# Summing a scan's states in pairs: one addition on GpSimd for every two transposes on TensorE, and all products with C on VectorE

## The chip, the cores and the metric

The kernel runs on one core of one Trainium2 chip. The time is device time in microseconds (us) of one execution, and the figure given is the median of several. An execution that the hardware profiler recorded is the source of everything said about single instructions; its page gives engines short names: PE for TensorE's matmuls, PEld for its weight loads, DVE for VectorE, ACT for ScalarE, POOL for GpSimd, SP for the engine that issues the DMAs.

## The reference, cut to what matters

Two layers of a network on x of shape (4, 512, 512). The change lies in layer 0's first half, a selective state-space scan with 512 channels, 512 time steps and 16 states:

```
delta = softplus(dt_proj_w @ dt_lo + dt_proj_b)       # per channel and time
def step(state, (d_t, B_t, C_t, u_t)):
    dA    = exp(d_t[..., None] * A)                   # A: channel x state
    state = state * dA + (d_t * u_t)[..., None] * B_t[:, None, :]
    y_t   = einsum('ben,bn->be', state, C_t)          # sum over the 16 states
y = (y + D * u) * silu(layernorm(x));   x = x + tanh(g_xattn[0]) * y^T
```

After it come a ternary feed-forward block ("bitnet"), cross attention with 16 heads, and four experts, each added to x behind its own gate.

## The kernel before, in words

**Batches and stages.** The four batch elements go through the kernel one behind the other. Batch 0's scan and bitnet run alone at the start. From then on the attention of batch b (16 heads, a head's query, score and weighted-sum steps staggered over three heads) is traced together with layer 0 of batch b+1, that is `front(b+1)`, `scan(b+1)` and `bitnet(b+1)`; a rate constant says how many steps of layer 0 come per step of attention. Beside the last batch's attention run the experts of batches 0 to 2, and the experts of batch 3 end the kernel. So there are four scan stages; in the last three attention shares every engine.

**Who sets the order.** The engines each work off a queue in order. The kernel's source is only traced: a scheduler at build time orders each engine's queue by priority (the order of tracing) and by when its own model of times expects operands and buffers to be there. A change in one place therefore moves instructions in others.

**The scan.** For a batch, 16 states n by four groups t of 128 channels make 64 tiles of 128 x 512 (channel by time). For each, `scan` (L606 to L686) does this: ScalarE writes dA = exp(delta * A) into a PSUM bank (L652); GpSimd writes h = (delta u) * B (`pool_mult`, L656, recorded at the helper's line L186); VectorE scans along time (L659 or L662); the state is multiplied by C, a row broadcast into the tile `cc`; and TensorE adds the product's transpose to y (`add`, four matmuls of 128x128 at L627 into PSUM tiles `py`). The choice of engine for the product with C:

```
if (G * n + t) % 8 in of_8:
    nc.vector.tensor_tensor_scan(dA, dA, h, 0.0, ALU.mult, ALU.add)
    nc.vector.tensor_tensor(h, dA, cc, ALU.mult)
else:
    nc.vector.tensor_tensor_scan(h, dA, h, 0.0, ALU.mult, ALU.add)
    pool_mult(h, h, cc)
```

With `DVE_OF_8` VectorE takes six products in eight (L660) and GpSimd two in eight (L186); batch 0 is called with `range(7)`, seven in eight, and with four channel groups at a time, the others with G = 2. In the first branch the state stays in PSUM until the product has read it; in the second the scan writes to SBUF, and dA's bank is free when the scan ends.

**Buffers.** `pss` has four PSUM banks; with G = 2 two hold `py`, so two are left for dA and for `psz`. SBUF tiles of 128 x 512 come from classes with the numbers of `MIDS`: class "v" holds h, and also tiles of `front`, the normalised rows, and in the last batch's attention the exponentials `pr`; class "t" holds the four tiles s1 of `front`'s softplus (L593), the skip term's tiles `udr` (L634, added to y after state 2), `zth` and `acc` of the scan, batch 0's `hq` and `xs`, and the rows `exr` of the early experts (L1158). A tile waits until the one that held its buffer has been read for the last time.

**Attention's small steps on GpSimd.** Between the scan's products stand the inverse square roots `rk` and `rqs` (`rsqrt`, L183), the low halves `ks` (L889) and some `hl` (L991), which keys and softmax wait for. VectorE's `hl` (L992) has two operands in SBUF.

Of the kernel before, what the change touches and what calls it, by code (L numbers as in the profile page):

```python
# [35 lines left out]
ALU = mybir.AluOpType  # L36
# [10 lines left out]
DS = 16  # L47
# [16 lines left out]
DVE_OF_8 = (0, 1, 2, 4, 5, 6)  # L64


MIDS = {"g": 5, "v": 6, "t": 4, "q": 2, "n": 1, "x": 1, "y": 2}
FILL0 = 4
RATE_S = 0.5
RATE_B = 0.8  # L70
# [21 lines left out]
SC = 4  # L92
PT = 3
MT = 0
AV = 4
VB = 2
WB = 5
# [13 lines left out]
def flamingo_kernel(  # L111
# [8 lines left out]
    nc = tc.nc  # L120
# [9 lines left out]
    pss = ctx.enter_context(tc.tile_pool(name="pss", bufs=4, space=PSUM))  # L130

    def psum(pool, name, tag="m", bufs=None):
        if tag == "a":
            role = name.rstrip("_0123456789")
            if pool is psa and role in LAST_PSS and name[len(role)] == str(B - 1):
                return psum(pss, name)
            tag = ATAG.get(role, "m")
            bufs = ABUF[tag]
        kw = {} if bufs is None else {"bufs": bufs}
        return pool.tile([P, 512], F32, tag=tag, name=name, **kw)  # L140
# [12 lines left out]
    def midt(shape, dtype, name, tag):  # L153
        if tag in wider:
            pool, bufs = wider[tag]
            return pool.tile(shape, dtype, tag=f"m{tag}", name=name, bufs=bufs)
        return mid.tile(shape, dtype, tag=tag, name=name, bufs=MIDS[tag])

# [18 lines left out]
    def load_x(b):  # L177
        x_sb[b] = xpool.tile([P, T, L], F32, tag="x", name=f"x{b}", bufs=2)
        nc.sync.dma_start(x_sb[b], x[b].rearrange("(p t) f -> p t f", t=T))
# [5 lines left out]
    def pool_mult(out, a, b):  # L185
        nc.gpsimd.tensor_tensor(out, a, b, ALU.mult)  # L186

    def row_stats(xr, name, gain=1.0, res=None):

        st = sm(6, f"bst{name[0]}", f"bst{name}", 2)  # L190
        nc.vector.bn_stats(st, xr)
        mv = sm(2, f"mv{name[0]}", f"mv{name}")
        nc.vector.bn_aggr(mv, st)
        var = sm(1, f"var{name[0]}", f"var{name}")
        nc.vector.tensor_scalar(var, mv[:, 1:2], EPS, gain**-2, ALU.add, ALU.mult)
        if res is None:
            res = sm(2, f"rst{name[0]}", f"rst{name}")
        rsqrt(res[:, 0:1], var)
        nc.vector.scalar_tensor_tensor(res[:, 1:2], mv[:, 0:1], -1.0, res[:, 0:1], ALU.mult, ALU.mult)
        return res  # L200

    def normed(xr, stats, name, tag="v"):
        xn = midt([P, L], F32, f"xn{name}", tag)
        if name[0] in NRMD:
            nc.vector.tensor_scalar(xn, xr, stats[:, 0:1], stats[:, 1:2], ALU.mult, ALU.add)
        else:
            nc.scalar.activation(xn, xr, AF.Identity, bias=stats[:, 1:2], scale=stats[:, 0:1])
        return xn
# [306 lines left out]
    def transposed(pool, src, name, g=None):  # L515

        ps = psum(pool, name).rearrange("p (t e) -> p t e", t=T)
        for t, s in enumerate(src):
            nc.tensor.transpose(ps[:, t, :], s[:, g::T], ident)
        return ps[:, : len(src), :]  # L520
# [82 lines left out]
            pool_mult(u[t], delta[t], u[t])  # L603
        yield

    def scan(b, of_8=DVE_OF_8, G=2, y_tile=lambda name: psum(pss, name), between=lambda n, ins: None):  # L606
        delta, du, ud_d, bd = fronts[b]
        sz_d = dram.tile([P, T, L], F32, tag="szd", name=f"szd{b}", bufs=2)

        def silu_z(t):  # L610

            xt = x_sb[b]
            w = normed(xt[:, t, :], row_stats(xt[:, t, :], f"z{b}{t}", 0.5), f"z{b}{t}")
            th = midt([P, L], F32, f"zth{b}{t}", "t")
            nc.scalar.activation(th, w, AF.Tanh)
            nc.vector.scalar_tensor_tensor(w, th, 1.0, w, ALU.add, ALU.mult)
            return w

        for t0 in range(0, T, G):
            gs = T // G
            ys = [y_tile(f"py{b}{t0}{i}").rearrange("p (g t e) -> p g t e", g=gs, t=G) for i in range(G)]

            def add(src, t, first, last):
                for g in range(T):
                    nc.tensor.matmul(  # L627
                        ys[g // gs][:, g % gs, t, :], src[:, g::T], ident, is_transpose=True,
                        start=first and t == 0 and g % gs == 0, stop=last, skip_group_check=True,
                    )  # L630

            uds, szs = [], []
            for t in range(G):
                uds.append(midt([P, L], F32, f"udr{b}{t0}{t}", "t"))  # L634
                nc.sync.dma_start(uds[t], ud_d[:, t0 + t, :])
            for n in range(DS):
                if n == 4 and x_sb[b] is None:
                    while b >= 2 and estats[b - 2] is None:
                        yield
                    load_x(b)  # L640
                if n == SZR and t0 > 0:
                    for t in range(t0, t0 + G):
                        szs.append(midt([P, L], F32, f"szr{b}{t}", "v"))
                        nc.sync.dma_start(szs[-1], sz_d[:, t, :])
                bc = midt([P, L], F32, f"bc{b}{t0}_{n}", "g")
                nc.sync.dma_start(bc, bd[n, :].partition_broadcast(P))
                cc = midt([P, L], F32, f"cc{b}{t0}_{n}", "g")
                nc.sync.dma_start(cc, bd[DS + n, :].partition_broadcast(P))
                for t in range(G):
                    nm = f"{b}{t0}{t}_{n}"  # L650
                    dA = psum(pss, f"dA{nm}")
                    last = nc.scalar.activation(  # L652
                        dA, delta[t0 + t], AF.Exp, scale=A[:, t0 + t, n : n + 1]
                    )
                    h = midt([P, L], F32, f"h{nm}", "v")
                    pool_mult(h, du[t0 + t], bc)  # L656
# [4 lines that stand above are left out]
                    else:  # L661
                        nc.vector.tensor_tensor_scan(h, dA, h, 0.0, ALU.mult, ALU.add)  # L662
                        pool_mult(h, h, cc)
                    add(h, t, n == 0, n == DS - 1)
                    if n == 2:
                        add(uds[t], t, False, False)
                between(n, last.ins)
                yield

            xt = x_sb[b]  # L670
            if t0 == 0:
                szs = [silu_z(t) for t in range(T)]
                for t in range(G, T):
                    nc.sync.dma_start(sz_d[:, t, :], szs[t])
            for g in range(T):
                if g % gs == 0:
                    acc = midt([P, gs, G, P], F32, f"acc{b}{t0}{g}", "t")
                    nc.scalar.copy(acc, ys[g // gs])
                ps = transposed(pss, szs[:G], f"psz{b}{t0}{g}", g)
                a = acc[:, g % gs]  # L680
                nc.vector.tensor_tensor(a, a, ps, ALU.mult)
                xv = xt[:, g, :].rearrange("q (p e) -> q p e", e=T)[:, :, t0 : t0 + G]
                nc.vector.scalar_tensor_tensor(
                    xv, a.rearrange("q e p -> q p e"), tg[:, 0:1], xv, ALU.mult, ALU.add
                )
                yield  # L686
# [139 lines left out]
    def attention(b):  # L826
# [70 lines left out]
        def values(hg):  # L897
            def v_tile(shape, dtype, name):
                return at.tile(shape, dtype, tag="v", name=name, bufs=AV)

# [270 lines left out]
    def last_experts(pool, places):  # L1171
# [12 lines left out]
        for t in (T - 1, *range(T - 1)):  # L1184
            xTs[t] = pool.tile([P, 2, T, P], F16, tag="v", name=f"lxT{t}", bufs=AV)
            split_normed(x_sb[b][:, t, :], estats[b][t], xTs[t], slice(0, P), f"l{t}", "q")
# [22 lines left out]
    with tc.tile_pool(name="pro", bufs=1) as pro, tc.tile_pool(name="psp", bufs=4, space=PSUM) as psp:  # L1209
# [8 lines left out]

        if MT:
            wider["t"] = pro, MT  # L1220

# [14 lines left out]
        def between(n, ins):  # L1236

            if n < 0:
                for _ in range(4):
                    next(side)  # L1240
            for _ in range(2 if 0 <= n < SIDE1 else 0):
                with tc.issue_after(ins):
                    next(side, None)

        run(front(0, inp, between))
        run(scan(0, range(7), 4, iter_ps, between))
        wider.clear()
        for _ in side:
# [50 lines left out]
    n = B * NH  # L1299
    for i in range(-2, n):  # L1300
        b2, h2 = divmod(i + 2, NH)
# [11 lines left out]
        q = steps[b2](h2, 0) if i + 2 < n else iter(())  # L1313
# [100 lines left out]
```

## Time and profile before

| what | value |
|---|---|
| median of three runs | 2029.95 us (2026.92 to 2033.11) |
| the profiled execution | 2033.82 us, span 2032.0 us |
| busy | PE 80%, DVE 76%, ACT 65%, POOL 46% of the span |
| mean granted TensorE clock | 0.877 |
| h products with B on POOL, L186 | 256 of 1327 ns |
| products with C on POOL, L186 | 56 of 1304 ns |
| products with C on DVE, L660 | 200 of 677 ns |
| scans on DVE | L659 200 of 1217 ns, L662 56 of 1207 ns |
| transposes of h on PE, L627 | 1024 of 341 ns, weight loads 1024 of 214 ns |

The scan's instructions lie from 50 to 200 us (batch 0), 380 to 600 (batch 1), 720 to 980 (batch 2) and 1100 to 1390 (batch 3). An instruction's mean duration is from its start to its end as recorded; neighbours on an engine overlap a little, so a group's sum can exceed the time that it takes. A wait is given as idle time of an engine before an instruction, with the instruction that ended it.

### The profile page before, as it was taken

How to read it: one execution, taken by the hardware profiler on the slowest of the kernel's cores; microseconds unless marked ns; L12 is line 12 of the kernel's file. 1: busy time of each engine (PE TensorE's matmuls, PEld its weight loads, DVE VectorE, ACT ScalarE, POOL GpSimd, SP SyncE). 2: the span in 40 equal slices, each digit the busy share in tenths (PEclk: the TensorE clock that was granted, in tenths of full speed). 3: DMA queues.
4: the chain of work that ended last, by engine and by line, in shares of the span. 5: the costliest groups of instructions: out<-in, count | busy, mean ns of one | idle time of the engine just before them, and what ended most of it. 6: DMA issues, size and time to landing. Idle time of an engine off the chain costs nothing. (4 is left out here: it accounts for less than half of the span.)

```text
span 2032.0 us, 27171 instructions
## 1 busy us (share of the span) xinstructions
PE 1634.5 (80%) x8366; PEld 901.1 (44%) x8366; DVE 1536.9 (76%) x2893; ACT 1328.6 (65%) x3121; POOL 937.3 (46%) x931
## 2 busy tenths in 40 slices
PE   4354976667879986779898887788999879798888
PEld 1343322344544444455443554554444445454456
DVE  4898865998998787898986885999764564654654
ACT  5797566765757886465658664756565676766763
POOL 1886112784744268475414782775133431412211
PEclk8555987768889998899999989899999889898989
DMA  7553558687884588775435777676445686866754
GB/s 258 185 161 133 151 158 242 185 228 218 231 214 107 132 216 182 191 177 155 106 87 149 199 180 191 156 170 146 91 103 111 139 228 158 210 160 165 193 138 140
DMA packets 516322, 342.50 MB, mean 169 GB/s; under 512 B 425800, under 2 KB 427976, under 8 KB 510032
## 3 DMA queue, kind: packets, MB, share of 16 engines
q1 hardware_dynamic: 516176, 340.77, 64.2%
q8 instruction: 65, 1.06, 0.2%
q14 instruction: 81, 0.66, 0.1%
HBM read 193.10 MB, written 44.30 MB: 117 GB/s over the span
## 5 line engine op out<-in xcount | busy, mean ns | idle before, releaser
L186 POOL TENSOR_TENSOR h<-u,bc 128x512 f32<-128x512 f32 x256 | 334.7, 1327 | 94.5 <-DMA bc<-bd 43.8
L627 PE MATMUL py<-ident,h 128*128 128x128 f32 x1024 | 201.1, 341 | 123.7 <-DVE h L660 101.9
L252 PE MATMUL ps<-kT,qT 128*128 128x512 f16 x768 | 217.0, 406 | 66.5 <-ACT pr L971 51.9
L652 ACT ACTIVATE dA<-delta,A 128x512 f32<-128x512 f32 x256 | 172.6, 685 | 138.8 <-DVE h L660 103.0
L659 DVE TENSOR_TENSOR_SCAN dA<-dA,h 128x512 f32<-128x512 f32 x200 | 240.8, 1217 | 23.5 <-POOL h L186 15.0
L252 PE MATMUL pav<-pT,v 128*128 128x256 f16 x1536 | 215.7, 297 | 46.2 <-DMA pT<-hl 28.9
L627 PEld LDWEIGHTS py<-ident,h 128*128 128x128 f32 x1024 | 167.6, 214 | 167.7 <-DVE h L660 131.0
L951 DVE TENSOR_REDUCE nmx<-ps 128x1 f32<-128x512 f32 x256 | 172.2, 679 | 54.9 <-PE ps L252 54.6
L971 ACT ACTIVATE pr<-ps,nmx,rqs 128x512 f32<-128x512 f32 x256 | 197.7, 775 | 20.8 <-DVE hl L992 16.6
L992 DVE SCALAR_TENSOR_TENSOR hl<-pr,den,hl 128x512 f16<-128x512 f32 x214 | 185.2, 882 | 33.4 <-ACT hl L989 17.0
L252 PEld LDWEIGHTS <-v 128*128 128x128 f16 x1536 | 161.7, 106 | 103.2 <-issue 44.2
L252 PE MATMUL pq<-axnT,wq 128*128 128x512 f16 x768 | 194.1, 404 | 7.7 <-DMA axnT<-xsa 3.1
L252 PE MATMUL pwo<-wo,oT 128*128 128x512 f16 x768 | 181.1, 386 | 8.6 <-DVE oT L244 3.6
L991 POOL TENSOR_SCALAR hl<-pr,den 128x512 f16<-128x512 f32 x86 | 66.3, 771 | 203.5 <-issue 97.5
L252 PEld LDWEIGHTS <-qT 128*128 128x128 f16 x768 | 77.8, 104 | 156.4 <-issue 88.6
L183 POOL TENSOR_TENSOR rqs<-ssq,mhalf 128x4 f32<-128x4 f32 x64 | 68.4, 1068 | 161.9 <-ACT ssq L940 149.0
L252 PEld LDWEIGHTS <-cT 128*128 128x128 f16 x768 | 79.1, 106 | 128.8 <-issue 61.7
L660 DVE TENSOR_TENSOR h<-dA,cc 128x512 f32<-128x512 f32 x200 | 133.7, 677 | 2.5 <-PE py L627 0.5
L252 PEld LDWEIGHTS <-wq 128*128 128x128 f16 x768 | 80.1, 105 | 108.3 <-issue 36.0
L252 PE MATMUL pk<-wk,cT 128*128 128x512 f16 x384 | 110.1, 432 | 19.9 <-DMA wk<-dwk 11.9
L252 PEld LDWEIGHTS <-oT 128*128 128x128 f16 x768 | 74.8, 100 | 100.6 <-issue 10.6
L989 ACT ACTIVATE hl<-pr,den 128x512 f16<-128x512 f32 x128 | 91.8, 717 | 36.3 <-DVE den L978 28.6
(386 smaller groups left out, 3478.2 us busy)
## 6 DMA issues: line engine op xcount, KB each, us to landing
bc<-bd SPq DMA_DIRECT2D x112, 256.0 KB
cc<-bd SPq DMA_DIRECT2D x112, 256.0 KB
wq<-dwq SPq DMA_DIRECT2D x64, 256.0 KB
wo<-dwo SPq DMA_DIRECT2D x64, 256.0 KB
w<-w3d SPq DMA_DIRECT2D x12, 1024.0 KB
de<-hle SPq DMA_DIRECT2D x9, 1024.0 KB
lw<-de SPq DMA_DIRECT2D x18, 512.0 KB
wk<-dwk SPq DMA_DIRECT2D x16, 512.0 KB
```

The costliest lines, as they stand in the source:

```text
L183: nc.gpsimd.tensor_tensor(res, arg, mhalf[:, : arg.shape[1]], ALU.pow)
L186: nc.gpsimd.tensor_tensor(out, a, b, ALU.mult)
L252: nc.tensor.matmul(ps, l, r, start=first and i == 0, stop=last and i == n - 1)
L627: nc.tensor.matmul(ys[g // gs][:, g % gs, t, :], src[:, g::T], ident, is_transpose=True, start=first and t == 0 and g % gs == 0, stop=last ...
L652: last = nc.scalar.activation(dA, delta[t0 + t], AF.Exp, scale=A[:, t0 + t, n : n + 1])
L659: nc.vector.tensor_tensor_scan(dA, dA, h, 0.0, ALU.mult, ALU.add)
L660: nc.vector.tensor_tensor(h, dA, cc, ALU.mult)
L951: nc.vector.tensor_reduce(nmx[:, c : c + 1], ps, AX.X, ALU.max, negate=True)
L971: mark[0] = nc.scalar.activation(pr, scs[c], AF.Exp, bias=nmx[:, one], scale=rqs[:, one], accum_out=den[:, c - c0 : c - c0 + 1],).ins
L989: nc.scalar.activation(hl[:, c, 0], prs[c], AF.Copy, scale=den[:, one])
L991: nc.gpsimd.tensor_scalar(hl[:, c, 0], prs[c], den[:, one], 1.0, ALU.mult, ALU.mult)
L992: nc.vector.scalar_tensor_tensor(hl[:, c, 1], prs[c], den[:, one], hl[:, c, 0], ALU.mult, ALU.subtract)
```

## The change

In batches 1 to 3 the products of states n = 2k and 2k+1 are kept for each channel group, GpSimd adds the second to the first, and TensorE transposes only the sum into y, 8 times per channel group instead of 16. The skip term is added after the second pair. `of_8` becomes `range(8)` for these batches, so that VectorE takes all products with C there. Batch 0 keeps its seven in eight and its single sums. Class "v" has seven buffers instead of six, class "t" three instead of four.

```diff
-MIDS = {"g": 5, "v": 6, "t": 4, "q": 2, "n": 1, "x": 1, "y": 2}
+MIDS = {"g": 5, "v": 7, "t": 3, "q": 2, "n": 1, "x": 1, "y": 2}
...
+PAIRS = (1, 2, 3)
...
-    def scan(b, of_8=DVE_OF_8, G=2, y_tile=lambda name: psum(pss, name), between=lambda n, ins: None):
+    def scan(b, of_8=range(8), G=2, y_tile=lambda name: psum(pss, name), between=lambda n, ins: None):
...
-            uds, szs = [], []
+            uds, szs, odd = [], [], [None] * G
...
-                    add(h, t, n == 0, n == DS - 1)
-                    if n == 2:
-                        add(uds[t], t, False, False)
+                    if b not in PAIRS:
+                        add(h, t, n == 0, n == DS - 1)
+                        if n == 2:
+                            add(uds[t], t, False, False)
+                    elif n % 2 == 0:
+                        odd[t] = h
+                    else:
+                        h2 = odd[t]
+                        nc.gpsimd.tensor_tensor(h2, h2, h, ALU.add)
+                        add(h2, t, n == 1, n == DS - 1)
+                        if n == 3:
+                            add(uds[t], t, False, False)
```

The lines of the changed kernel behind the constants lie one lower, behind this block ten lower; the addition is at L673.

## The prediction

> **What bounds the kernel now.** I read the page first for each engine's share, then the busy time of the three stretches in which a scan of batches 1 to 3 runs beside attention, then the waits inside them, then a few single rows. The page says that no engine is full over the whole span:
>
> ```profile
> PE 1634.5 (80%) x8366; PEld 901.1 (44%) x8366; DVE 1536.9 (76%) x2893; ACT 1328.6 (65%) x3121; POOL 937.3 (46%) x931
> L627 PE MATMUL py<-ident,h 128*128 128x128 f32 x1024 | 201.1, 341 | 123.7 <-DVE h L660 101.9
> L660 DVE TENSOR_TENSOR h<-dA,cc 128x512 f32<-128x512 f32 x200 | 133.7, 677 | 2.5 <-PE py L627 0.5
> ```
>
> That average mixes stages. The busy times of the scan stretches of batches 1, 2 and 3 (columns: stretch, its length, then busy us of PE, PEld, DVE, ACT, POOL, the granted clock, the DMA share, GB/s):
>
> ```profile
> 380.00:600.00 220.00, 160.89 (x797) 102.81 (x795) 207.06 (x320) 143.37 (x360) 143.16 (x123) 0.78 0.82 223
> 720.00:980.00 260.00, 206.68 (x1108) 127.98 (x1107) 221.20 (x356) 168.35 (x423) 175.97 (x160) 0.90 0.73 179
> 1100.00:1390.00 290.00, 235.30 (x1241) 140.85 (x1239) 239.05 (x382) 184.28 (x467) 184.97 (x169) 0.91 0.74 180
> ```
>
> VectorE leads in each: 94%, 85% and 82% of the stretch, against TensorE's 73%, 79% and 81%. Only the first is clearly VectorE's. The bitnet stretches between them are TensorE's (118.4 of 120 us from 600 to 720 us), but no transposes of h stand there. The waits in the first stretch, of TensorE, VectorE and GpSimd:
>
> ```profile
> PE py L627 <- DVE h L660: 21.5, 11, 5.8
> POOL h L186 <- PE py L627: 18.8, 7, 7.3
> POOL h L186 <- DVE h L662: 18.7, 8, 4.3
> PE ps L252 <- ACT pr L971: 15.7, 5, 5.8
> ...
> DVE nmx L951 <- PE ps L252: 9.3, 7, 3.1
> ```
>
> TensorE stands in its queue before a transpose whose product VectorE hasn't finished, with attention's matmuls behind it; and most of VectorE's little idle time (9.3 of 12.9 us) is spent on scores that come late.
>
> **The change, part by part.** *Products with C.* 48 of them (16 per stage) go from GpSimd to VectorE, each 677 ns by L660, so 10.8 us per stage and 32.5 us in all. How much of it ends up on the path I take from VectorE's share of each stage: 10.8 x (0.94 + 0.85 + 0.82) = +28.2 us. The bounds are 0, if its idle time took everything, and +32.5 us.
>
> *Transposes.* 384 matmuls with their weight loads go, 128 per stage (256 become 128; the skip term's stay). Their recorded mean of 341 ns overlaps with neighbours; back to back the trace has this:
>
> ```profile
> 513.39 2.08 PE L627 MATMUL py<-ident,h 128*128 128x128 f32 x16
> ```
>
> That is 0.13 us for one, so 16.6 us per stage, 49.9 us in all; by the 341 ns it would be 43.7 us per stage, of which most is waiting inside the group. I take 16.6, since the instructions that follow get only this. It counts where VectorE isn't the one that is late, that is in VectorE's idle share, 6%, 15% and 18%: 16.6 x 0.39 = -6.5 us. Half as many places where TensorE stands before a transpose also bring scores earlier. VectorE waited for scores 9.3, 3.7 and 6.9 us in the three stages; half of these 19.9 us makes -10 us (bounds 0 and -19.9).
>
> *GpSimd.* It gains 96 additions and loses 48 products. No addition of two such SBUF tiles stands in the scan; the nearest row is its product of the same shape, 1327 ns. 96 x 1.327 - 48 x 1.304 = +64.8 us, 21.6 per stage: from 143 to 165 of 220 us, from 176 to 198 of 260, from 185 to 207 of 290. The cover is its idle time, 77 us in the first stage. An addition waits for VectorE's product, as the products at L186 waited for L662 (18.7, 5.0 and 14.0 us in the three stages, 37.7 us over 48, 0.79 us each). Behind a waiting addition stand the next h products, `rk`, `rqs` and `ks`, which keys and softmax wait for. There is a second cost: VectorE's `hl` with both operands in SBUF sometimes takes a GpSimd instruction longer, the first stage's row being:
>
> ```profile
> L992 DVE SCALAR_TENSOR_TENSOR hl<-pr,den,hl x29: 721/741/1753, 379.3 to 595.4; 128x512 f16<-128x512 f32 x29
> ```
>
> The mean of these 29 is 928 ns, 187 above their median, 5.4 us in the stage; 15% more GpSimd work makes about 1 us more per stage. I take +5 us for all of this, between 0 and the 75.8 us that 96 waits of 0.79 would be if nothing covered them. The chosen value is near the lower end since these waits were largely covered before.
>
> *dA's bank.* With the product on VectorE a bank is free one product later, 48 times 0.677 = 32.5 us of later exponentials at worst. VectorE waited for dA at L659 or L662 only 1.1, 2.3 and 1.2 us in the three stages, so the two banks are enough so far: +3 us.
>
> *Batch 0.* Its code is the same, but with a seventh tile its queue changes: GpSimd now has eight h products ahead of four long weight steps (`wst`, together 7.8 us) where it had three. VectorE stood here once for 7.07 us:
>
> ```profile
> 74.25 1.23 DVE L659 TENSOR_TENSOR_SCAN dA<-dA,h 128x512 f32<-128x512 f32 x1 [7.07 <-POOL h L186]
> ```
>
> Five more products of 1.27 us let VectorE work on meanwhile; I take half of the gap, -3.5 us (-7 to +3, since GpSimd is busy 118 of 150 us there and the weight steps come later).
>
> *Class "t" with three tiles.* `front`'s fourth s1 waits until the first has been used up. In the new queue of ScalarE this makes four more loads of function tables, 1.28 us each, on an engine that is 65% busy; the early experts load one row less ahead, and batch 0's `hq` and `xs` share three tiles where TensorE waited for `hqT` 3.0 us. The seventh "v" tile may help `pr` in the last batch. Together +2 us, between -5 and +12.
>
> The sum: 28.2 - 6.5 - 10 + 5 + 3 - 3.5 + 2 = +18.2 us. The profiled execution took 2033.8 us (1.8 us beside its span), 3.9 above the median, so 2052 for such an execution and **2048 us** for the median.
>
> **Two rules of the Trainium skill.** The trace's granted clock was 0.53 from 50 to 200 us, where TensorE was busy 72 of 150 us, 0.78 in the first scan stage, and 1.00 from 600 to 720 us, where it was busy throughout. In the Trainium skill ("TensorE: Matmul & The Clock Gate", Part 1) the clock is halved after an idle window of about 3.4 us and released by sustained work. By that rule thinning out the transposes would lower the clock of attention's matmuls: if 0.78 became 0.70 in the first stage, its other 111 us of matmuls would grow by up to 12 us. My sum has nothing for this, since TensorE is idle 59 us there, and I keep it at that.
>
> GpSimd's product takes 1327 ns, VectorE's 677. "GPSIMD Engine Reference" (4.1, Engine selection) has two-input elementwise work on VectorE, GpSimd being about twice as slow. By it the additions belong on VectorE: 96 x 0.677 = 65 us more on the engine that leads these stages, a sum near +70. Here the stage's fullest engine counts, not the single instruction, so I hold the additions to be on the right engine and the products to be on the wrong one.
>
> **The rivals.** *TensorE's relief decides (28%).* In stages 2 and 3 TensorE's share is within 6 points of VectorE's, and its queue holds up all the others. If these two stages end with it, they gain 2 x 16.6 = 33.2 us; stage 1 still pays 10.1, GpSimd 5, batch 0 gives 3.5: -21.6, so about 2008 us. For it: VectorE's 38.8 and 51.0 us of idle time there. Against it: the products come on VectorE in the same places. It decides if VectorE's idle time takes up the 10.8 us.
>
> *GpSimd's queue comes late (17%).* If the 96 additions wait as L662's followers did, GpSimd stands 75.8 us instead of 37.7; half of the additional 38 us passing on to softmax and keys adds 19 to the sum: 2067 us. It decides once VectorE's waits for h or `rk` exceed their few us of before (in stage 1 0.3 for h).
>
> *They cancel (10%).* With 28 us of relief in place of 16.5 the sum is within some 6 us of nothing. The change does do what it says: the queues hold 384 transposes of h fewer, 48 more products on VectorE and 96 additions.
>
> **The numbers.** My forecast (45%) has its own range of 2036 to 2065. With TensorE's relief on one side and GpSimd's lateness on the other, the range is 2005 to 2080: below it half of what is better than the first rival, above it the costs of "t", the bank and GpSimd together. A difference of 0.3% (6 us) is about the least that a measurement of this kernel can tell from no change. Faster 0.28, within 0.3% 0.10, slower 0.62.
>
> **What would show it.** Right: VectorE above 95% in the stage of batch 1 and each scan stage some 3 to 12 us longer, the bitnet stretches alike, TensorE's waits for h about halved. Wrong: scan stages of batches 2 and 3 shorter with VectorE at 90% or more; or VectorE waiting for GpSimd's h or `rk` for tens of us; or a difference that arises outside the scan stages, in batch 0 or in the last batch's attention.

## The result and the profile after

The changed kernel took 2048.0 us (median of seven runs, 2038.3 to 2055.1) where the kernel before took 2029.95 (seven runs, 2026.9 to 2033.1). The ratio is 1.0081 with a 95% interval of 1.006 to 1.0102: slower by some 16 us. The profiled execution, at 2040.4 us, is at the fast end of its runs, so its trace holds only a third of the difference; prices below therefore come from ratios, and the trace tells where things lie.

The page of the changed kernel, for the rows shown of before:

```profile
PE 1583.6 (78%) x7982; PEld 843.3 (41%) x7982; DVE 1589.4 (78%) x2941; ACT 1336.2 (66%) x3125; POOL 1004.8 (49%) x979
...
L1002 DVE SCALAR_TENSOR_TENSOR hl<-pr,den,hl 128x512 f16<-128x512 f32 x214 | 205.6, 977 | 23.7 <-POOL hl L1001 14.8
...
L628 PE MATMUL py<-ident,h 128*128 128x128 f32 x640 | 131.2, 348 | 98.2 <-DVE h L661 46.3
...
L661 DVE TENSOR_TENSOR h<-dA,cc 128x512 f32<-128x512 f32 x248 | 167.0, 680 | 4.6
L673 POOL TENSOR_TENSOR h<-h,h 128x512 f32<-128x512 f32 x96 | 130.1, 1357 | 67.9 <-DVE h L661 50.2
```

TensorE is 51 us less busy, VectorE 52.5 us more, of which the 48 products make only 33 (167.0 us for L661, 133.7 before). GpSimd's additions cost 1357 ns each, and GpSimd stood 67.9 us before them, mostly for VectorE's product. The three stretches of before, same windows and columns:

```profile
380.00:600.00 220.00, 137.09 (x645) 80.75 (x646) 215.84 (x318) 141.44 (x355) 163.15 (x134) 0.77 0.81 213
720.00:980.00 260.00, 189.63 (x952) 106.39 (x951) 235.01 (x346) 162.07 (x400) 191.08 (x169) 0.89 0.74 179
1100.00:1390.00 290.00, 224.24 (x1098) 121.06 (x1097) 243.03 (x382) 189.49 (x452) 205.61 (x182) 0.89 0.73 178
```

VectorE is at 98% in the first window. From the first to the last scan instruction on VectorE, stage 1 took 225 us (before 210), stage 2 230 (221), stage 3 258 (256). The waits from 380 to 600 us:

```profile
PE py L628 <- POOL h L673: 23.1, 10, 9.4
...
POOL h L673 <- DVE h L661: 21.1, 11, 4.2
ACT pr L981 <- DVE hl L1002: 11.8, 7, 6.3
```

TensorE's wait for VectorE's product (21.5 us) has been replaced by one just as long for GpSimd's addition, in 10 places, one of 9.4 us, and the additions in turn wait for VectorE. The other two rows shown before, VectorE's low halves `hl` in the first stretch and its wait in batch 0:

```profile
L1002 DVE SCALAR_TENSOR_TENSOR hl<-pr,den,hl x30: 720/1177/1848, 383.7 to 599.7; 128x512 f16<-128x512 f32 x30
```

```profile
79.45 1.23 DVE L660 TENSOR_TENSOR_SCAN dA<-dA,h 128x512 f32<-128x512 f32 x1 [4.79 <-POOL h L187]
```

`hl`'s median in this window went from 741 to 1177 ns. Over the kernel its mean is 977 ns instead of 882, 20.4 us for 214 of them: the rest of VectorE's additional busy time. The row of before:

```profile
L992 DVE SCALAR_TENSOR_TENSOR hl<-pr,den,hl 128x512 f16<-128x512 f32 x214 | 185.2, 882 | 33.4 <-ACT hl L989 17.0
```

That made collisions with GpSimd the first suspect.

### The profile page after: what moved, and what is told of

It is laid out like the page before. It is cut to its first block, busy times and chain, and to the rows that moved or that the text cites. A ratio compares the mean times of both kernels' runs of the same rounds, so it can differ in the third digit from the quotient of the medians.

```text
span 2038.6 us, 26422 instructions
## 1 busy us (share of the span) xinstructions
PE 1583.6 (78%) x7982; PEld 843.3 (41%) x7982; DVE 1589.4 (78%) x2941; ACT 1336.2 (66%) x3125; POOL 1004.8 (49%) x979
## 5 line engine op out<-in xcount | busy, mean ns | idle before, releaser
L660 DVE TENSOR_TENSOR_SCAN dA<-dA,h 128x512 f32<-128x512 f32 x248 | 299.9, 1218 | 13.4 <-POOL h L187 8.2
L253 PE MATMUL pav<-pT,v 128*128 128x256 f16 x1536 | 210.4, 290 | 63.2 <-DMA pT<-hl 35.7
L253 PE MATMUL pq<-axnT,wq 128*128 128x512 f16 x768 | 207.4, 424 | 39.4 <-DVE ksq L890 19.2
L1002 DVE SCALAR_TENSOR_TENSOR hl<-pr,den,hl 128x512 f16<-128x512 f32 x214 | 205.6, 977 | 23.7 <-POOL hl L1001 14.8
L961 DVE TENSOR_REDUCE nmx<-ps 128x1 f32<-128x512 f32 x256 | 173.0, 679 | 59.5 <-PE ps L253 59.2
L628 PE MATMUL py<-ident,h 128*128 128x128 f32 x640 | 131.2, 348 | 98.2 <-DVE h L661 46.3
L253 PE MATMUL pwo<-wo,oT 128*128 128x512 f16 x768 | 186.2, 393 | 20.5 <-DVE oT L245 9.0
L661 DVE TENSOR_TENSOR h<-dA,cc 128x512 f32<-128x512 f32 x248 | 167.0, 680 | 4.6
L673 POOL TENSOR_TENSOR h<-h,h 128x512 f32<-128x512 f32 x96 | 130.1, 1357 | 67.9 <-DVE h L661 50.2
L628 PEld LDWEIGHTS py<-ident,h 128*128 128x128 f32 x640 | 108.1, 214 | 131.0 <-DVE h L661 59.8
L973 ACT ACTIVATE nmx<-nmx,rqs 128x1 f32<-128x1 f32 x256 | 69.6, 293 | 77.8 <-DVE nmx L961 51.7
```

The lines of the kernel that those rows point to most:

```text
L253: nc.tensor.matmul(ps, l, r, start=first and i == 0, stop=last and i == n - 1)
L628: nc.tensor.matmul(ys[g // gs][:, g % gs, t, :], src[:, g::T], ident, is_transpose=True, start=first and t == 0 and g % gs == 0, stop=last ...
L673: nc.gpsimd.tensor_tensor(h2, h2, h, ALU.add)
L961: nc.vector.tensor_reduce(nmx[:, c : c + 1], ps, AX.X, ALU.max, negate=True)
L973: nc.scalar.activation(nmx[:, one], nmx[:, one], AF.Copy, scale=rqs[:, one])
L1002: nc.vector.scalar_tensor_tensor(hl[:, c, 1], prs[c], den[:, one], hl[:, c, 0], ALU.mult, ALU.subtract)
```

## The experiments

Each kernel was timed beside the kernel before on its chip; what is compared is the ratio to it. The four h kernels were timed on another chip than the e and f kernels; the kernel before took 2028.96 us there and 2025.21 beside the f kernels. The chip of the change itself isn't known, and none of the twelve was timed on both, so a difference between an h kernel and one of the others may hold an error that its interval doesn't show. "v" and "t" are the numbers of tiles of the two classes.

| kernel | v, t | products on VectorE | sums | ratio, 95% interval |
|---|---|---|---|---|
| before | 6, 4 | 6 of 8 | single | 1 |
| the change | 7, 3 | all | pairs | 1.0081, 1.006 to 1.0102 |
| e1_pairs_6of8 | 7, 3 | 6 of 8 | pairs | 1.0051, 1.0032 to 1.0069 |
| e2_products_only | 6, 4 | all | single | 0.9996, 0.9978 to 1.0014 |
| e3_tiles_only | 7, 3 | 6 of 8 | single | 0.9955, 0.9935 to 0.9974 |
| e4_add_one_column | 7, 3 | all | pairs, one column added | 1.0007, 0.9985 to 1.0029 |
| f1_tiles_products | 7, 3 | all | single | 0.9986, 0.9966 to 1.0006 |
| f2_even_states_only | 7, 3 | all | odd states left out | 0.9973, 0.9951 to 0.9996 |
| f3_pairs_on_vector | 7, 3 | all | pairs, added on VectorE | 1.0142, 1.011 to 1.0174 |
| f4_class_t_only | 6, 3 | 6 of 8 | single | 0.9944, 0.9926 to 0.9961 |
| h1_one_input_passes | 7, 3 | all | pairs, two copies for the sum | 1.0069, 1.0042 to 1.0096 |
| h2_pairs_v6 | 6, 3 | all | pairs | 0.9981, 0.9965 to 0.9997 |
| h3_v6_t3_products | 6, 3 | all | single | 0.9874, 0.9845 to 0.9903 |
| h4_skip_later | 6, 4 | 6 of 8 | single | 1.0009, 0.9987 to 1.0032 |

**First four: the parts of the change.** *e1_pairs_6of8* puts the products back:

```diff
-    def scan(b, of_8=range(8), G=2, ...
+    def scan(b, of_8=DVE_OF_8, G=2, ...
```

> The change with VectorE's share of the products with C put back to six in eight: GpSimd has the 96 additions and all of its old 48 products. Theory A (VectorE's added instruction time sets it: 32.5 us of products, and about 20 us by which its two-SBUF-operand low halves hl are stretched beside GpSimd's additions): the products' 32.5 us go, the stretch of hl stays or grows, time between 2025 and 2040 us, hl's mean 977 ns or above. Rival B (GpSimd's queue is what comes late): GpSimd gets 63 us more, so slower than the change, 2055 us or more, with VectorE waiting for h from GpSimd by tens of us. Rival C (the tile classes cost it): as the change, 2043 to 2053 us.

2036.8 us beside 2026.8: inside theory A's numbers and outside the two rivals', but with a step that is a fifth of A's. The products cost 0.30 ± 0.28% here (6 us), not 32.5 us, and GpSimd's 63 us more did no harm. `hl`'s mean stayed at 976 ns, as A had it.

*e2_products_only* is the same edit the other way, on the kernel before.

> The kernel before with all products with C of batches 1 to 3 on VectorE, no pairs, no additions, old tile classes. Theory A: 32.5 us of products come, against which hl is stretched less, since GpSimd has 63 us less two-input work: hl's mean from 882 to some 830 ns (11 us), so 2035 to 2052 us. Rival B: GpSimd's queue is relieved, so 2030 us or less. Rival C: no tiles are touched, 2030 us.

2026.84 us beside 2026.82. The forecast's largest term, 28 us for the products, is nothing here; the numbers of B and C came. Its groups on GpSimd and VectorE:

```profile
L186 POOL TENSOR_TENSOR h<-u,bc 128x512 f32<-128x512 f32 x256 | 337.1, 1334 | 138.8 <-PE py L627 86.9 <-DMA bc<-bd 39.5 <-DVE ksq L880 2.6
```

```profile
L992 DVE SCALAR_TENSOR_TENSOR hl<-pr,den,hl 128x512 f16<-128x512 f32 x214 | 185.7, 884 | 36.4 <-ACT hl L989 21.2 <-POOL hl L991 14.5 <-POOL pr L984 0.3
```

GpSimd, rid of 48 products and the waits for their scans, now runs ahead until it has no free tile, 86.9 us of waiting for transposes (42.0 before). One reading is that the products' time is paid on VectorE and given back by a GpSimd that isn't late any more; no run shows that by itself. That `hl` would be stretched less was wrong, its mean is 884 ns.

*e3_tiles_only* changes only `MIDS`.

> The kernel before with seven tiles of class v and three of class t, nothing else. Theory A: the forecast's terms for batch 0 (-3.5 us) and for class t (+2), so 2022 to 2035 us. Rival B: the same. Rival C: most of the 18 us, 2040 us or more.

2019.5 us, 9 us less than before: more than A had (its lower end is just passed), and C's sign is wrong.

*e4_add_one_column* shortens the additions and leaves every wait; the sums leave out the other 511 columns:

```diff
-                        nc.gpsimd.tensor_tensor(h2, h2, h, ALU.add)
+                        nc.gpsimd.tensor_tensor(h2[:, 0:1], h2[:, 0:1], h[:, 0:1], ALU.add)
```

> The change with GpSimd adding only the first of the 512 columns of each pair, so that the sums leave out the other columns; every wait, transpose and tile stays, the additions' 1.27 us becomes a fraction of it. Theory A: the stretch of hl goes back to or below that of before (mean 880 ns or less) and GpSimd's 122 us go: about 20 us less than the change, 2022 to 2034 us. Rival B by its waits (an addition waits for VectorE's product, however short it is): 2040 us or more. Rival C: 2043 to 2053 us.

2027.5 us, ratio 1.0007: of the change's 0.81% the additions' duration is 0.74 ± 0.30%, as A had it. `hl`'s mean is 913 ns; A's 880 was missed.

```profile
L673 POOL TENSOR_TENSOR h<-h,h 128x1 f32<-128x1 f32 x96 | 24.3, 255 | 92.9 <-DVE h L661 81.3 <-DVE den L988 4.4 <-DVE p2cwq L218 2.5
```

```profile
L1002 DVE SCALAR_TENSOR_TENSOR hl<-pr,den,hl 128x512 f16<-128x512 f32 x214 | 190.7, 913 | 25.8 <-POOL hl L1001 14.7 <-ACT hl L999 10.7 <-POOL pr L994 0.3
```

**Second four: the pairs taken apart.** *f1_tiles_products* is e2 with tiles 7 and 3.

> The change without its pairs: tile classes 7 and 3, all products with C of batches 1 to 3 on VectorE, every h transposed by itself. What the first four runs suggest (theory D: products are free once GpSimd's 48 two-input products go in exchange, the tiles give about 9 us, and the pairs alone cost some 25): 2013 to 2023 us beside a before of about 2027. The forecast's own term (theory A, 28 us for the products): 2035 us or more. The difference between this run and the change is the price of the pairs, with TensorE's relief in it.

Ratio 0.9986 (2024.3 us, a little above D's band, far from A's). The change without its pairs is no slower than before, so the pairs cost 0.95%.

*f2_even_states_only* drops the addition's line, so that the odd states are left out of the sums.

> The change without the additions: only the even states' products are transposed, the odd ones are computed and left out of the sum. So TensorE has its relief of 384 matmuls and nobody waits for an addition. Theory D (the pairs' price is the additions' time on GpSimd and the waits for them, and relief is worth little but not less than nothing): at or below the change without pairs, 2003 to 2020 us. Rival E (thinned-out transposes cost time by themselves, by a lower granted clock or another order): above the change without pairs, 2022 us or more.

2018.1 us, within D's numbers. TensorE's relief alone is worth 0.13% with an uncertainty of 0.30%: nothing that can be told. From here to the change it is 0.34 ± 0.31% for the additions' waits, with an instruction of 255 ns each (e4 less f2), and 0.74 ± 0.30% for the rest of their duration (the change less e4).

*f3_pairs_on_vector*:

```diff
-                        nc.gpsimd.tensor_tensor(h2, h2, h, ALU.add)
+                        nc.vector.tensor_tensor(h2, h2, h, ALU.add)
```

> The change with the 96 additions on VectorE in place of GpSimd. Theory D: 96 x 0.68 = 65 us more for VectorE in the stages that it leads, and as two-SBUF-operand instructions beside GpSimd's h products some of them stretched by up to 1 us, against which GpSimd loses 127 us and hl's stretch falls below that of the change: 2050 to 2090 us. The rule that two-input elementwise work belongs on VectorE: less than the change, 2040 us or less.

2055.3 us, inside D's numbers: 0.6% (12 us) above the additions on GpSimd. An addition took 805 ns on VectorE.

*f4_class_t_only* is `"v": 6, "t": 3` on the kernel before.

> The kernel before with three tiles of class t and the old six of class v. Theory D has the seventh v tile as the gain (h products ahead in batch 0, and pr in the last batch) and class t as a small loss: 2027 to 2037 us, so that the seventh tile is worth 8 us or more. Rival: the other order that comes with three t tiles is the gain, 2022 us or less.

2012.7 us, ratio 0.9944: D was wrong. The seventh tile gives nothing here (0.11 ± 0.26% more in e3); what gains is one tile less of class "t".

**Last four.** *h1_one_input_passes*: is the additions' duration paid by collisions on VectorE, or in GpSimd's queue? Two copies of the odd state's product take the addition's place, and the even state is left out of the sum.

```diff
-                        nc.gpsimd.tensor_tensor(h2, h2, h, ALU.add)
+                        for _ in range(2):
+                            nc.gpsimd.tensor_scalar(h2, h, 1.0, 1.0, ALU.mult, ALU.mult)
```

> The change with each addition replaced by two one-input passes on GpSimd that copy the odd state's product (the even state's is left out of the sum). GpSimd is occupied as long as by the additions, or longer (its one-input instructions of this shape took 0.62 to 0.77 us, so 1.25 to 1.5 us for two), and the waits are the same; what goes is the two-input instruction beside which VectorE's hl is stretched. Theory F (collision: the additions' time costs by stretching VectorE's two-SBUF-operand instructions): hl's mean 920 ns or less, 2022 to 2034 us, ratio to the kernel before 1.004 or less. Theory G (queue: the additions' time costs by keeping the h products and the root steps behind them waiting): as the change or slower, ratio 1.007 or more.

```profile
L674 POOL TENSOR_SCALAR h<-h 128x512 f32<-128x512 f32 x192 | 131.2, 688 | 78.8 <-DVE h L661 64.2 <-DVE varz L196 3.6 <-DVE den L989 3.6
```

```profile
L1003 DVE SCALAR_TENSOR_TENSOR hl<-pr,den,hl 128x512 f16<-128x512 f32 x214 | 192.7, 919 | 32.4 <-ACT hl L1000 17.6 <-POOL hl L1002 14.2 <-POOL pr L995 0.3
```

GpSimd is occupied just as long as by the additions (131.2 us against 130.1), and `hl` is down to 919 ns, so that 13 of the 20 us of stretch are gone. The ratio of 1.0069 lies outside F's numbers, just below G's, and 0.12 ± 0.34% (2 ± 7 us) below the change. The comparison with e4 says more: `hl` is nearly the same there (913 ns), GpSimd is occupied for 24.3 us instead of 131.2, and the time is 0.62 ± 0.35% (13 ± 7 us) less. So the price of the duration is that of GpSimd's queue. The stretched `hl`, which had looked like the whole loss, cost little; some us of it are not excluded.

*h2_pairs_v6* is the change with six tiles of class "v".

> The change with six v tiles in place of seven, class t still three: what the seventh tile is worth to the pairs. If the pairs need it (four h tiles of a pair of states are held at once, so only two are left to run ahead): 8 us or more above the change, ratio 1.012 or more. If it is worth as little as to single sums (tiles alone 0.9955 with seven, 0.9944 with six): ratio 1.006 to 1.010.

Neither: 2025.4 us beside 2029.0, ratio 0.9981. The seventh tile of class "v" makes the pairs slower, by 1.0%.

*h3_v6_t3_products* is f1 with six tiles.

> The best version so far (class t at three, nothing else) with all products with C of batches 1 to 3 on VectorE. By the two prices of the products so far (0 with the old tiles, 0.3% with 7 and 3): ratio 0.994 to 0.998. Theory A's 28 us would make it 1.008. If GpSimd's 63 us less two-input work outweighs the products: below 0.994.

2006.7 us beside 2029.0, ratio 0.9874: the third of the cases expected (below 0.994), and faster than both kernels. Again 1.1% lies between six tiles and seven. VectorE's wait for scores, over the whole kernel, in the kernel with seven tiles (f1) and the one with six (h3):

```profile
DVE nmx L951 <- PE ps L252: 77.5, 55, 5.9
```

```profile
DVE nmx L951 <- PE ps L252: 46.4, 42, 6.1
```

31 us less with six. In the pairs it is 59.2 us with seven tiles (the change) and 39.2 with six (h2). These differences are about as large as those of the times (f1 to h3 22 us, the change to h2 20 us); with six in eight products on VectorE, where the seventh tile costs nothing that can be told (0.11%), the wait isn't longer with seven (49.4 against 55.6). It would fit a scheduler that puts h products ahead of attention's steps when it has a tile for them, so that scores come late.

Three things in the traces speak against this reading. Over the other kernels the wait doesn't follow the time: it is 45.9 us in e2 (ratio 0.9996), 45.6 in f3 (1.0142) and 60.9 in f2 (0.9973). Of the 31 us only 7 lie between the first and the last scan instruction of a batch (18.2 us in f1, 11.6 in h3), of the 20 us in the pairs 12. And the scan stages took no longer with seven tiles: 211, 220 and 255 us in f1 against 215, 224 and 257 in h3, and 225, 230 and 258 in the change against 235, 238 and 253 in h2. Why the seventh tile costs time stays open.

*h4_skip_later* gauges how much an order drawn anew moves by itself:

```diff
-                    if n == 2:
+                    if n == 3:
                         add(uds[t], t, False, False)
```

> The kernel before with the skip term added after state 3 instead of state 2, as the change has it for its pairs: the same work, only its place and the time that two t tiles are held differ. By its work: ratio 0.998 to 1.002. If it lies outside, then an order that the scheduler draws anew moves the time by as much as the smaller differences measured here, and those can't be put down to an instruction's price.

1.0009: nothing. One such gauge doesn't prove that an order never moves the time by more. What speaks for the prices is that they come again: three couples of kernels give nearly the same for the pairs (0.95, 1.07 and 0.96%), two for the seventh tile (1.00 and 1.12%). Class t by itself (-0.56%) and the products with six tiles and t at three (-0.70%) were measured once each, and there a new order remains a possible cause.

## Why the prediction was right, and where it wasn't

The direction was right, and the number was right by luck: its terms weren't, and their errors made up for each other. The forecast's mechanism, VectorE paying for the products, is not what the runs show. Two ratios subtracted, with their half intervals joined by squares, give each part's price; 1% is 20.3 us.

| part | where measured | price |
|---|---|---|
| class t, 4 to 3 | f4 | -0.56 ± 0.18% |
| products, six v tiles | h3 less f4 (t 3); e2 (t 4) | -0.70 ± 0.34%; -0.04 ± 0.18% |
| products, seven v tiles | f1 less e3; the change less e1 | +0.31 ± 0.28%; +0.30 ± 0.28% |
| pairs | the change less f1; h2 less h3; e1 less e3 | +0.95 ± 0.29%; +1.07 ± 0.33%; +0.96 ± 0.27% |
| seventh v tile, all products on VectorE | the change less h2; f1 less h3 | +1.00 ± 0.26%; +1.12 ± 0.35% |
| seventh v tile, 6 of 8 | e3 less f4 | +0.11 ± 0.26% |

One path from before to the change, each step measured in what the step before left: class t -11 us, products -14, pairs +22, seventh tile +20, together +16 us. (The last two steps and the products use h kernels; an error between the chips would move products and seventh tile in opposite directions and leave the sum.) The forecast had, for the same four, +2, +31.2 (products and dA's bank), -11.5 (the transposes' two terms and GpSimd's) and -3.5. So it was 45 us too high in the second and 13 in the first, 33 and 24 us too low in the other two.

*Products, +28.2 us.* This term failed. The step was the weighting by VectorE's busy share: a share of 94% was taken for a 94% chance that an added microsecond is late. Measured is between -14 and +6 us. The 63 us that GpSimd lost were only set off against its additions; that h products come earlier without them had no term. They do, as far as e2's and h3's waits tell: GpSimd stood 86.9 and 102.7 us for transposes to free a tile, 42.0 before. The signs that the prediction named came in part, VectorE at 98% in the stage of batch 1 and the scan stages 15, 9 and 2 us longer; but e2, which is no slower, has a first stage of 225 us too, with VectorE busy for 209.5 of the 220 us.

*Transposes, -6.5 and -10 us.* Measured -2.6 ± 6 us without any addition (f2 less f1); the larger of the two terms, earlier scores, is not seen: VectorE's wait for scores rose from 54.6 to 59.2 us in the whole kernel. The waits in front of transposes weren't halved but taken over by the additions.

*GpSimd, +5 us.* The term that was mis-sized: measured is 22 us (the change less f2). The value was taken near its lower end because the earlier waits had been covered. The additions stood 67.9 us, near the 75.8 of the bound, and the cover was gone, since TensorE now waited behind them (29.6 us for L673 in the whole kernel, a release that was not there before). The mechanism is that of the second rival, GpSimd's queue, whose 19 us on top of the 5 were about the right size; VectorE's own waits for h, which were to show it, did not rise (8.2 us for L660 in the whole kernel, 15.0 before), nor, beyond 1.5 us, those for `rk` (25.6 and 24.1). The collisions, put at 3 us, were 20 us of busy time; h1 took 13 of them away, and the time moved by 2 ± 7 us.

*dA's bank, +3 us.* VectorE waited for dA 4.6 us in the whole kernel; 8.1 before. Nothing, as far as can be seen.

*Batch 0, -3.5 us.* The wait fell from 7.07 to 4.79 us, about as worked out, but not because of the seventh tile: with six tiles and t at three (f4) seven h products already stand ahead of the weight steps, and the wait is as short:

```profile
78.65 1.22 DVE L662 TENSOR_TENSOR_SCAN h<-dA,h 128x512 f32<-128x512 f32 x1 [4.53 <-POOL h L186]
```

The scan there ended at 185 instead of 183 us and bitnet at 306 instead of 298, in f4 at 183 and 301. The sign was wrong; that the weight steps, 5 us later on GpSimd, put off others is a reading. By itself this delay doesn't set the time: in f1, which is no slower than before, bitnet ended at 310. The 20 us that the seventh tile costs with all products on VectorE were in no term.

*Class "t", +2 us.* -11 us, outside its bounds of -5 to +12. The four additional table loads came (40 instead of 36, 1.28 us each), and the time fell all the same. Why fewer tiles help stays open: in the trace of f4 bitnet of batches 1, 2 and 3 ends 9, 16 and 12 us earlier, and no single wait was found that accounts for it.

*The two rules.* The granted clock fell in the three stages from 0.78, 0.90 and 0.91 to 0.77, 0.89 and 0.89, in the direction of the Trainium skill's "TensorE: Matmul & The Clock Gate" (Part 1), by far less than the 0.08 put to it. "GPSIMD Engine Reference" (4.1) would have the additions on VectorE; measured, that is 12 ± 8 us slower than on GpSimd, with the sign that the rows gave and a fifth of their 65 us. What the rows missed is that the additions are best on neither, and that the products, which the forecast held to be on the wrong engine, cost nothing on VectorE with six tiles.

## What to carry to other kernels

A busy share is not the price of an added microsecond (28 us forecast, -14 to +6 measured): ask what the engine that loses work will do earlier. An operation that makes one engine wait for a second and a third for the first costs by its place in the queue, even where its engine is half idle; leaving out its duration (one column) and then the wait itself tells the two apart. Change numbers of buffers by themselves and in both directions: here the two edits that looked like mere accommodation were worth -11 and, with all products on VectorE, +20 us, and of the kernels run the version without the pairs and the seventh tile is the fastest.

## What the runs showed of the hardware

VectorE's low halves, with two operands in SBUF, took longer beside a two-input instruction of GpSimd. Of the 214 in the changed kernel's trace, 77 began while GpSimd ran a two-input 128x512 instruction and took 1.35 us in the mean, 110 began with GpSimd idle and took 0.74 us, none over 0.76. The product L661, which has one operand in PSUM, took 0.68 us in both cases. The Trainium skill's "GPSIMD Engine Reference" (1, Specifications) names this contention for VectorE instructions with two SBUF inputs, and the rows agree. What was unexpected is how little it cost on the busiest engine of these stages: with 13 of the 20 us gone (h1) the time moved by 2 ± 7 us.
